# Graph layer with scattered sums: the last partial sums joined on VectorE, and the node stage in five lagged stages in source order

## The chip, the cores and the metric

The kernel runs on one core of a Trainium2 chip. A core has TensorE (PE) for matrix products, VectorE (DVE), ScalarE (ACT) and GpSimd (POOL) for element work, SyncE (SP), whose queue here only issues transfers, and 16 DMA engines that all queues share. Matrix products land in PSUM, everything else on the core lies in SBUF, and the tables of rows lie in device memory. The engines run side by side, each in the order of its own instructions, and wait for one another on semaphores. The metric is the device time of one execution in microseconds (us), as the median of several runs.

## The reference

One graph layer over 6,250 nodes with 64 features and 206,250 directed edges with 64 attributes: an MLP for each edge, the mean of its results at each edge's first node, an MLP for each node, a residual connection and a layer norm without weights.

```
msg  = concat([x[col], edge_attr])            # edges x 128
h    = relu(msg @ W1a.T + b1a) @ W1b.T + b1b  # 128 hidden, 64 out
agg  = segment_sum(h, row) / max(count, 1)
z    = relu(concat([x, agg]) @ W2a.T + b2a) @ W2b.T + b2b
out  = layernorm(x + concat([z, x]) @ Wr.T + br)
```

Everything is float32. `W1b` is linear and comes after the ReLU, so the kernel sums the 128 hidden values per node and folds `W1b`, `W2b` and `Wr` into combined weights (`wam_t`, `wzz_t`).

## The kernel before, in words

Nodes are split into 49 bins of 128 (the last has 106 nodes). Edges come in 124 blocks of 13 x 128. For each block PE forms the hidden values (line 949), ACT applies the ReLU (line 950), and POOL scatters the rows with 13 indirect DMAs (line 956) into a table in device memory that is sorted by bin. A row is 130 floats: 128 hidden values, a one that becomes the count, and the number of the node within its bin. A tile is 128 such rows.

The blocks are grouped into five epochs of 82, 17, 14, 7 and 4 blocks, each with a table of its own (three buffers in turn). When an epoch, or a step of the first one, is complete, its rows are read back (`read`, line 1000, on SP's queue, nine buffers `rt` in turn). DVE compares each row's node number with a ramp to form a one-hot matrix (`nodes_of`, lines 1031 and 1034), and PE multiplies one-hot by rows and so sums the rows of each node in PSUM (`summed`, line 1052). `sum_next` (line 1112) does this for a group of up to three bins: it sums the group, forms the next group's one-hot, and lets `collect` (line 1102) add all but the newest finished group into the SBUF array `part` with one DVE instruction (line 1110). The sums of the fourth epoch (seven blocks, three tiles per bin, two bins per group) are what is left after the last scatter, before the last step.

The last step (`last`, the fifth epoch) is treated in another way. Its bins have two tiles each, read three bins at a time. `sum_last` forms the one-hot and calls `summed` with `last` true. There the earlier sum of a bin is put into PSUM by an identity matmul ahead of the two tiles (line 1050), each bin in a PSUM tile of its own, so that PSUM ends with the complete sum. `finish` then takes over bin by bin: copy of the count (line 1286), reciprocal of the count (1288, 1289), scaling on ACT (1290), transpose on PE (1291). Every fourth bin `nodes` does the rest for four bins: copy of the transposed block on ACT (1299), the product with `wam_t` (1301), a maximum with the negated part that was computed long before (1302; that is the ReLU), four products with `wzz_t` (1305), the addition of the residual (1309), statistics (1313, 1314), square root on ACT (1316), reciprocal and offset (1317, 1319), normalisation on ACT (1323) and the output DMA on ACT's queue (1328, 1332).

Order: up to the end of the fourth epoch's sums, PE, ACT, DVE and SP run in source order (`in_order`, a manual schedule). The last step lies behind `in_order.close()`, where a planner orders each engine's instructions by its own estimates. Instructions behind the close that don't depend on the last step, such as the checks of line 805, are placed earlier by it. The checks end in `flag` (line 1373), which every engine loads before the kernel's last branch (lines 1427, 1428).

PSUM pools around the change: `spp` has two tiles for sums, `hp` three, which all node-stage products share in turn. The pool `nw` for the node stage's SBUF tiles has two of each.

Of the kernel before, what the change touches and what calls it, by code (L numbers as in the profile page):

```python
# [8 lines left out]
F32 = mybir.dt.float32  # L9
# [8 lines left out]
P = 128  # L18
# [459 lines left out]
def fast_path(  # L478
# [199 lines left out]
    with (  # L678
# [364 lines left out]
        def summed(st, reads, oh, of_bin, done):  # L1043

            last, at_tile = st is steps[-1], 0
            for b0, nb, t0, n, rt in reads:
                for j in range(nb):
                    b = b0 + j
                    if last and t0 == st.lo[b]:
                        nc.tensor.matmul(of_bin(b), ident, part[:, b, :], start=True, stop=False)  # L1050
                    for t in range(n):
                        nc.tensor.matmul(  # L1052
                            of_bin(b), oh[:, at_tile, :], rt[:, j * n + t, : H + 1],
                            start=t0 + t == st.lo[b] and not last, stop=t0 + t == st.hi[b] - 1,
                        )
                        at_tile += 1
                    if t0 + n == st.hi[b]:
                        done(b)
# [53 lines left out]
        def sum_next():  # L1112
# [5 lines left out]
            summed(g.st, g.reads, g.oh, lambda b: g.ps[:, b - g.b0, :], lambda b: None)  # L1118
            totals.append(g)
            mark()  # L1120
            collect(1)

# [147 lines left out]
        collect(0)  # L1270
        in_order.close()
# [4 lines left out]
        cnt_all = const.tile([P, NB], F32, name="cnt_all")  # L1276
        by_slot.close()
        with tc.tile_pool(name="nw", bufs=2) as nw:
            pending = []

            def finish(b, ps):
                if not pending:
                    pending.append((b, nw.tile([P, SUB, H], F32, name="agg"), hp.tile([P, SUB * P], F32, name="h_ps")))
                b0, agg, tr = pending[0]
                j = b - b0
                nc.vector.tensor_copy(cnt_all[:, b : b + 1], ps[:, H:])
                rc = nw.tile([P, 1], F32, name="rc")
                nc.vector.tensor_scalar(rc, ps[:, H:], 1.0, None, op0=ALU.max)
                nc.vector.reciprocal(rc, rc)
                nc.scalar.activation(agg[:, j, :], ps[:, :H], AF.Copy, scale=rc)  # L1290
                nc.tensor.transpose(tr[:, j * P : (j + 1) * P], agg[:, j, :], ident)
                if j == SUB - 1 or b == NB - 1:
                    nodes(b0, j + 1, tr)
                    pending.clear()

            def nodes(b0, n, tr):
                cols = slice(b0 * P, (b0 + n) * P)
                aT = nw.tile([P, SUB * P], F32, name="aT")
                nc.scalar.copy(aT[:, : n * P], tr[:, : n * P])
                p1 = hp.tile([P, SUB * P], F32, name="h_ps")  # L1300
                nc.tensor.matmul(p1[:, : n * P], wam_t, aT[:, : n * P], start=True, stop=True)  # L1301
                nc.vector.tensor_max(nq[:, cols], nq[:, cols], p1[:, : n * P])
                p3 = hp.tile([P, SUB, D], F32, name="h_ps")
                for j in range(n):
                    nc.tensor.matmul(  # L1305
                        p3[:, j, :], nq[:, (b0 + j) * P : (b0 + j + 1) * P], wzz_t, start=True, stop=True
                    )
                y = nw.tile([P, SUB, D], F32, name="y")
                nc.vector.tensor_add(y[:, :n, :], p3[:, :n, :], xr[:, b0 : b0 + n, :])
                st = nw.tile([P, SUB, 6], F32, name="st")  # L1310
                mvr = nw.tile([P, SUB, 2], F32, name="mvr")
                for j in range(n):
                    nc.vector.bn_stats(st[:, j, :], y[:, j, :])
                    nc.vector.bn_aggr(mvr[:, j, :], st[:, j, :])
                rstd = nw.tile([P, SUB], F32, name="rstd")
                nc.scalar.activation(rstd[:, :n], mvr[:, :n, 1], AF.Sqrt, bias=eps)
                nc.vector.reciprocal(rstd[:, :n], rstd[:, :n])
                off = nw.tile([P, SUB], F32, name="off")
                nc.vector.scalar_tensor_tensor(
                    off[:, :n], mvr[:, :n, 0], -1.0, rstd[:, :n], op0=ALU.mult, op1=ALU.mult  # L1320
                )
                for j in range(n):
                    nc.scalar.activation(  # L1323
                        y[:, j, :], y[:, j, :], AF.Identity, bias=off[:, j : j + 1], scale=rstd[:, j : j + 1]
                    )
                full = min(n, NF - b0)
                if full > 0:
                    nc.scalar.dma_start(
                        out[b0 * P : (b0 + full) * P].rearrange("(b p) f -> p b f", p=P), y[:, :full, :]
                    )  # L1330
                if full < n:
                    nc.scalar.dma_start(out[NF * P :], y[:REM, full, :])

            def sum_last():
# [96 lines left out]
```

## Time and profile before

| what | value |
|---|---|
| median of 9 runs | 2597.91 us (2587.15 to 2603.98) |
| the profiled execution | 2602.78 us |
| its span, first to last instruction | 2601.0 us |
| mean granted TensorE clock | 0.721 |
| busy PE / DVE / ACT / POOL | 1458.3 / 1181.4 / 327.0 / 1560.6 us |
| last scatter on POOL starts | 2452.47 us |
| first identity matmul (line 1050) | 2501.17 us |
| last output is issued (line 1332) | 2596.37 us |

Times inside the profile count from the start of the span. A line of a group view reads: source line, engine, operation, output<-inputs, shapes and count | busy us, mean ns of one | idle time of the engine just before them and what ended it. A line of the waits reads: who waited <- for whom: us in total, times, longest. A line of windows gives, for a stretch, the busy us of each engine with its instruction count, the granted TensorE clock (1.00 is full), the busy share of the DMA engines, and GB/s. In the page's slices each digit is a tenth. PE's float32 matmuls have two records each; PE's ends are modelled, so distances between starts say more than the lengths.

### The profile page before, as it was taken

To read this page: it belongs to the slowest core of one execution; us is meant where nothing else is said; L and a number is where in the kernel's file an instruction comes from. 1 tells how busy PE (TensorE), PEld (TensorE's weight loads), DVE (VectorE), ACT (ScalarE), POOL (GpSimd) and SP (SyncE) were. 2 spreads that over 40 slices of the span, in tenths; PEclk is the share of its full clock that TensorE was granted. 3 is DMA by queue.
4 is the path that set the end of the run, shared out by engine and by line. 5 is a ranking of instruction groups with operands and counts; after the bars stand their busy time and mean duration, and the time that the engine had idled before them with its cause. 6 is when DMAs were issued, how large, how long until landed. Compare 5 with 4: busy or idle time off the path is not lost.

```text
span 2601.0 us, 25280 instructions
## 1 busy us (share of the span) xinstructions
PE 1458.3 (56%) x8343; PEld 1277.3 (49%) x8343; DVE 1181.4 (45%) x2072; ACT 327.0 (13%) x799; POOL 1560.6 (60%) x1630
## 2 busy tenths in 40 slices
PE   3545553345545444544545566656656565667786
PEld 3434442344545334443444555555555554656775
DVE  5233343343443433344344444564554553555575
ACT  1111111101111101101110111111001010101024
POOL 6566666666666666666666666656666665665400
PEclk8666666666767766666667777776777776777799
DMA  7467655534444443433444555544555563555561
GB/s 169 132 224 255 171 161 162 154 115 114 135 117 130 119 113 114 125 115 112 135 119 123 149 152 147 161 134 139 149 147 152 150 173 111 159 164 170 183 186 29
DMA packets 198721, 375.23 MB, mean 144 GB/s; under 512 B 47034, under 2 KB 113916, under 8 KB 198452
## 3 DMA queue, kind: packets, MB, share of 16 engines
q1 hardware_dynamic: 114806, 222.07, 31.6%
q0 software_dynamic: 51584, 107.40, 13.1%
q10 hardware_dynamic: 32190, 44.05, 5.3%
q8 instruction: 68, 1.11, 0.2%
q14 instruction: 73, 0.60, 0.1%
HBM read 221.77 MB, written 151.59 MB: 144 GB/s over the span
## 4 chain that ended last, share of the span: by engine, by line
PE 26%; issue 16%; another core or an unknown queue 9%; DVE 5%; DMA 1%; ACT 1%; SPq 1%; ACTq 0%; DVEq 0%
PE sum_ps L1052 13%; PE h_ps L949 9%; DVE oh L1034 2%; DMA rt<-rows 1%; PE cnt_ps L851 1%; PE cnt_ps L850 1%; DVE rhs L929 1%; PE h_ps L1301 1%; DVE part L1110 1%; ACT y L1323 0%; PE h_ps L1305 0%; ACT orow L950 0%; DVE had L837 0%; DVE row L867 0%
## 5 line engine op out<-in xcount | busy, mean ns | idle before, releaser
L956 POOL DMA_INDIRECT rows<-orow,rowidx x1612 | 1552.7, 963 | 892.2 <-issue 457.0
L949 PE MATMUL h_ps<-mv,rhs 128*128 128x128 f32 x3224 | 632.5, 349 | 469.7 <-issue 339.0
L949 PEld LDWEIGHTS h_ps<-mv,rhs 128*128 128x128 f32 x3224 | 574.9, 259 | 535.2 <-issue 382.9
L1052 PE MATMUL sum_ps<-rt,oh 128*128 128x129 f32 x4006 | 621.9, 310 | 272.0 <-issue 247.3
L1052 PEld LDWEIGHTS sum_ps<-rt,oh 128*128 128x128 f32 x4006 | 578.4, 224 | 297.6 <-issue 272.3
L950 ACT ACTIVATE orow<-h_ps 128x512 f32<-128x512 f32 x496 | 248.9, 519 | 2069.8 <-remote 1191.6
L1034 DVE TENSOR_TENSOR oh<-ramp,rt 128x512 f32<-128x512 f32 (+3 forms) x213 | 144.9, 703 | 559.6 <-DMA rt<-rows 402.8
L929 DVE TENSOR_TENSOR rhs<-rhs,ramp 64x1664 f32<-64x1664 bf16 x116 | 219.4, 1892 | 20.3 <-DMA rhs<-relt 12.0
L837 DVE TENSOR_TENSOR_SCAN had<-ramp,bins 128x700 bf16<-128x700 bf16 x124 | 200.3, 1615 | 4.3
L1110 DVE TENSOR_TENSOR part<-part,sum_ps 128x258 f32<-128x258 f32 (+2 forms) x166 | 77.2, 465 | 269.3 <-remote 166.7
L850 PE MATMUL cnt_ps<-had,one_w 128*128 128x350 bf16 x248 | 100.2, 407 | 175.1 <-issue 87.9
L1034 DVE TENSOR_TENSOR oh<-ramp,node 128x512 f32<-128x512 f32 (+3 forms) x237 | 187.1, 790 | 7.3
L867 DVE TENSOR_REDUCE row<-cnt_ps 128x14 f32<-128x700 f32 x124 | 109.1, 880 | 105.9 <-issue 47.7
L1031 DVE SCALAR_TENSOR_TENSOR node<-unused,rt 128x4 f32<-128x4 bf16 (+3 forms) x237 | 37.4, 160 | 194.8 <-DMA rt<-rows 145.0
L851 PEld LDWEIGHTS <-before_w 128*128 128x128 bf16 x248 | 29.0, 117 | 196.8 <-issue 184.8
L851 PE MATMUL cnt_ps<-bins,before_w 128*128 128x325 bf16 x248 | 102.0, 414 | 37.0 <-issue 36.9
L831 DVE TENSOR_TENSOR bins<-ramp,hi 128x650 bf16<-128x650 f32 x124 | 108.2, 873 | 0.0
L850 PEld LDWEIGHTS <-one_w 128*128 128x128 bf16 x248 | 29.8, 120 | 74.7 <-issue 65.1
L1158 DVE TENSOR_SCALAR zT<-h_ps 128x512 f32<-128x512 f32 (+1 forms) x13 | 8.6, 661 | 121.1 <-remote 68.5
L1153 PE MATMUL h_ps<-zT,w2x_t 65*128 65x512 f32 (+1 forms) x26 | 20.4, 881 | 64.0 <-ACT orow L950 35.4
L830 DVE TENSOR_TENSOR bins<-had,ramp 128x50 bf16<-128x50 bf16 x119 | 44.1, 371 | 2.7
L1162 PE MATMUL h_ps<-nwzz_t,zT 128*128 128x64 f32 x98 | 22.5, 404 | 35.5 <-DVE zT L1158 20.7
(115 smaller groups left out, 445.2 us busy)
## 6 DMA issues: line engine op xcount, KB each, us to landing
rt<-rows SPq DMA_DIRECT2D x242, 260.0 KB
rhs<-in_edgeT SPq DMA_DIRECT2D x124, 416.0 KB
rt<-rows SPq DMA_DIRECT2D x106, 390.0 KB
rows<-orow,rowidx POOLq DMA_INDIRECT x1612
rhs<-relt SPq DMA_DIRECT2D x116, 208.0 KB
rows<-padrow ACTq DMA_DIRECT2D x4, 4680.0 KB
rows<-padrow ACTq DMA_DIRECT2D x8, 2340.0 KB
rt<-rows SPq DMA_DIRECT2D x48, 325.0 KB
```

Source lines behind the costliest of these rows:

```text
L831: nc.vector.tensor_tensor(by_bin[:, :, 1:], ramp[:, : 2 * HALF, None].to_broadcast([P, 2 * HALF, BLK]), hi[:, None, c0 : c0 + BLK].to_broa ...
L837: nc.vector.tensor_tensor_scan(had, on, oh, 0.0, op0=ALU.mult, op1=ALU.add)
L850: nc.tensor.matmul(v, one_w, had[:, b, :], start=True, stop=False)
L851: nc.tensor.matmul(v[:, :, :BLK], before_w, oh[:, b, 1:], start=False, stop=True)
L867: nc.vector.tensor_reduce(row, v.rearrange("p i b t -> p t i b"), axis=mybir.AxisListType.XY, op=ALU.max)
L929: nc.vector.tensor_tensor(rhs[D:, :].rearrange("p (h e) -> p h e", h=2), rel, in_win[D:, :, None].to_broadcast([WIN, 2, NG * P // 2]), op= ...
L949: nc.tensor.matmul(ps[:, j, :], rhs[:, c * P : (c + 1) * P], m, start=True, stop=True)
L950: nc.scalar.activation(orow[:, k0 : k0 + n, :H], ps[:, :n, :], AF.Relu)
L956: s = nc.gpsimd.indirect_dma_start(out=ep_.rows, out_offset=bass.IndirectOffsetOnAxis(ap=rowidx[:, t : t + 1], axis=0), in_=orow[:, j, :], ...
L1034: nc.vector.tensor_tensor(res[:, at_tile : at_tile + nb * n, :], ramp[:, None, :].to_broadcast([P, nb * n, P]), node[:, :, None].to_broadc ...
L1052: nc.tensor.matmul(of_bin(b), oh[:, at_tile, :], rt[:, j * n + t, : H + 1], start=t0 + t == st.lo[b] and not last, stop=t0 + t == st.hi[b] ...
L1110: nc.vector.tensor_add(to, to, g.ps[:, : g.nb, :])
```

## The change

The last step uses the same path as all others. `summed` loses the identity matmul, and `sum_next`, which now returns its group, sums the group's three bins in one PSUM tile; `collect` adds them to `part` with one DVE instruction for three bins. The reads of the last step go through `issue` and `to_issue` as all others do.

The node stage becomes a class `Nodes` with five methods for one group of up to three bins. Iteration i of the loop sums group i, collects group i-1, and then calls `means` for group i-1, `turned` for i-2, `layer` for i-3, `residual` for i-4 and `written` for i-5. `in_order.close()` moves behind this loop, so PE, ACT, DVE and SP take all of it in source order. The counts are read from `part` (three at a time for the reciprocals, all 49 at once for the final check). `nw` gets three buffers of each tile in place of two, and the outputs go to SP's queue.

```diff
-        def summed(st, reads, oh, of_bin, done):
+        def summed(st, reads, oh, of_bin):
...
-                    if last and t0 == st.lo[b]:
-                        nc.tensor.matmul(of_bin(b), ident, part[:, b, :], start=True, stop=False)
...
-                    if t0 + n == st.hi[b]:
-                        done(b)
...
             collect(1)
+            return g
...
-        collect(0)
-        in_order.close()
...
-        with tc.tile_pool(name="nw", bufs=2) as nw:
...
+        with tc.tile_pool(name="nw", bufs=3) as nw:
+            class Nodes:
...
+                def means(self):
+                    rc = nw.tile([P, SUMS], F32, name="rc")[:, : self.nb]
+                    nc.vector.tensor_scalar(rc, part[:, self.bins, H], 1.0, None, op0=ALU.max)
+                    nc.vector.reciprocal(rc, rc)
+                    self.agg = nw.tile([P, SUMS, H], F32, name="agg")
+                    for j in range(self.nb):
+                        nc.scalar.activation(
+                            self.agg[:, j, :], part[:, self.b0 + j, :H], AF.Copy, scale=rc[:, j : j + 1]
+                        )
+
+                def turned(self):
+                    tr = hp.tile([P, SUMS * P], F32, name="h_ps")
+                    for j in range(self.nb):
+                        nc.tensor.transpose(tr[:, j * P : (j + 1) * P], self.agg[:, j, :], ident)
+                    self.aT = nw.tile([P, SUMS * P], F32, name="aT")[:, : self.nb * P]
+                    nc.scalar.copy(self.aT, tr[:, : self.nb * P])
+
+                def layer(self):
+                    p1 = hp.tile([P, SUMS * P], F32, name="h_ps")[:, : self.nb * P]
+                    nc.tensor.matmul(p1, wam_t, self.aT, start=True, stop=True)
+                    nc.vector.tensor_max(nq[:, self.cols], nq[:, self.cols], p1)
+
+                def residual(self):
+                    p3 = hp.tile([P, SUMS, D], F32, name="h_ps")
+                    for j in range(self.nb):
+                        b = slice((self.b0 + j) * P, (self.b0 + j + 1) * P)
+                        nc.tensor.matmul(p3[:, j, :], nq[:, b], wzz_t, start=True, stop=True)
+                    y = self.y = nw.tile([P, SUMS, D], F32, name="y")
+                    nc.vector.tensor_add(y[:, : self.nb, :], p3[:, : self.nb, :], xr[:, self.bins, :])
...
+                    for j in range(self.nb):
+                        nc.vector.bn_stats(st[:, j, :], y[:, j, :])
+                    for j in range(self.nb):
+                        nc.vector.bn_aggr(self.mvr[:, j, :], st[:, j, :])
+
+                def written(self):
...
+                    nc.scalar.activation(rstd[:, :n], mvr[:, :n, 1], AF.Sqrt, bias=eps)
+                    nc.vector.reciprocal(rstd[:, :n], rstd[:, :n])
...
+                    for j in range(n):
+                        nc.scalar.activation(
+                            y[:, j, :], y[:, j, :], AF.Identity, bias=off[:, j : j + 1], scale=rstd[:, j : j + 1]
+                        )
...
+                        nc.sync.dma_start(
+                            out[b0 * P : (b0 + full) * P].rearrange("(b p) f -> p b f", p=P), y[:, :full, :]
+                        )
...
+            to_issue += [(last, g) for g in groups_of(last)]
+            n_last, on_way = len(to_issue), []
+            for i in range(n_last + 5):
+                issue(NGR)
+                if i < n_last:
+                    on_way.append(Nodes(sum_next()))
+                else:
+                    collect(0)
+                issue(NGR)
+                for lag, stage in enumerate(("means", "turned", "layer", "residual", "written"), 1):
+                    if 0 <= i - lag < n_last:
+                        getattr(on_way[i - lag], stage)()
+            in_order.close()
...
+            cnt_all = nw.tile([P, NB], F32, name="cnt_all")
+            nc.vector.tensor_copy(cnt_all, part[:, :, H])
```

## The prediction

> **What bounds the kernel now.** I read the page's slices first, to see which stage the change touches. A slice is 65.0 us.
>
> ```profile
> PE   3545553345545444544545566656656565667786
> ...
> POOL 6566666666666666666666666656666665665400
> PEclk8666666666767766666667777776777776777799
> ```
>
> Up to slice 38 the scatter on POOL runs without a break, and nothing in the diff reaches that part: the built order of POOL is the same in both kernels, and PE, DVE, ACT and SP differ there only in line numbers and in where a few small checks of 0.2 us sit. POOL's last scatter starts at 2452.47. All the change can do lies after it, and that stretch I read by windows (columns: bounds, length, busy us of PE, PE loads, DVE, ACT, POOL with counts, granted clock, DMA share, GB/s).
>
> ```profile
> 2456.00:2501.00 45.00, 43.75 (x365) 43.07 (x364) 41.69 (x110) 0.00 (x0) 0.00 (x0) 0.97 0.91 289
> 2501.00:2516.00 15.00, 10.43 (x74) 8.55 (x73) 8.44 (x51) 6.06 (x15) 0.00 (x0) 1.00 0.44 123
> 2516.00:2546.00 30.00, 23.22 (x159) 18.98 (x159) 18.93 (x111) 14.05 (x42) 0.00 (x0) 1.00 0.38 90
> 2546.00:2576.00 30.00, 23.93 (x152) 19.24 (x152) 17.87 (x103) 13.26 (x40) 0.00 (x0) 0.94 0.09 19
> ```
>
> From 2456 to 2501 the sums of the fourth epoch fill PE (97%) and DVE (93%): a full stage, which the change leaves alone. From 2501 PE is busy 77%, DVE 63%, ACT 47%, DMA below half: no engine is full. That is the last step, sums plus node stage. It runs from the first identity matmul (2501.17) to the issue of the last output (2596.37), 95.2 us for 49 bins. The starts of the square root, one per four bins, give its pace: 2521.76 to 2588.99 over nine periods, 7.47 us per four bins, 1.87 us per bin. What fills a period that no engine fills is the view of waits:
>
> ```profile
> DVE cnt_all L1286 <- PE sum_ps L1052: 13.1, 18, 1.4
> DVE zT L1302 <- PE h_ps L1301: 12.9, 11, 2.4
> ACT rstd L1316 <- DVE rc L1288: 11.2, 7, 1.8
> PE h_ps L1291 <- ACT agg L1290: 10.8, 12, 1.6
> ```
>
> PE waits for ACT, ACT for DVE, DVE for PE: one group of four goes through its whole chain with little of the next beside it. The last step is bound by hand-overs.
>
> **The change, part by part.** One period now handles three bins: 16 periods, and one for bin 48.
>
> *Removed.* The 98 records of the identity matmul (49 fp32 matmuls, two records each), and 49 each of the copy, the maximum and the reciprocal on DVE:
>
> ```profile
> L1034 DVE TENSOR_TENSOR oh<-ramp,node 128x768 f32<-128x768 f32 x15 | 14.2, 948 | 0.0
> ...
> L1289 DVE RECIPROCAL rc<-rc 128x1 f32<-128x1 f32 x49 | 7.7, 157 | 0.7
> L1286 DVE COPY cnt_all<-sum_ps 128x1 f32<-128x1 f32 x49 | 7.2, 147 | 13.1 <-PE sum_ps L1052 13.1
> ...
> L1110 DVE TENSOR_TENSOR part<-part,sum_ps 128x387 f32<-128x387 f32 x1 | 0.6, 560 | 0.3 <-PE sum_ps L1052 0.3
> ```
>
> *PE per period.* In the timeline four records of the sum take 0.45 us before the next begins, so 6 tiles, 12 records, 1.35. Three transposes at 0.11 make 0.35. The 512-column layer takes 0.96 until the next, so 384 columns 0.72. Six records of the residual at 0.118 make 0.70. Sum 3.1 us (before, the identity matmuls added 0.22 a bin).
>
> *DVE per period*, in issue order, each by the distance to the next start in the timeline: node places 0.20, one-hot 0.87, the added sum 0.56 plus 0.04 until its dependent starts, maximum and reciprocal 0.19 + 0.16. The layer's maximum has 128x384, between 0.69 (128x512) and 0.26 (128x128); nearest the first, 0.55, next start after 0.47. The residual's add 128x192, between 0.42 and 0.23, taken 0.36, dependent after 0.40. Three statistics and three aggregates 0.65 (four pairs took 0.87). Reciprocal and offset 0.40. Sum 3.94 us. So DVE, not PE, is the fullest engine; before, DVE had 63% of 5.6 us for three bins, 3.5 us: the added sum costs more than the copies that go.
>
> *ACT per period.* It adds nothing and loses the output DMAs. But source order makes a chain in one period: the reciprocal's start on DVE at 0.20 + 0.87 + 0.60 + 0.19 = 1.86; the mean starts 0.26 later (2579.21 to 2579.47), 2.12; three means 0.27 apart, 2.93; copy of the turned block, 384 columns, 0.49 of the 0.59 for 512, 3.42; square root, and its reciprocal on DVE 0.33 after its start (2593.12 to 2593.45), 3.75; the offset 0.21 later, 3.96; the next period's first DVE instruction about 0.1 after that. The last of these steps as the timeline has them before (start, length, engine):
>
> ```profile
> 2593.12 0.30 ACT L1316 ACTIVATE rstd<-mvr,eps 128x4 f32<-128x4 f32 x1 [1.07 <-DVE mvr L1314]
> ...
> 2593.45 0.18 DVE L1317 RECIPROCAL rstd<-rstd 128x4 f32<-128x4 f32 x1 [0.19 <-ACT rstd L1316]
> 2593.66 0.16 DVE L1319 SCALAR_TENSOR_TENSOR off<-mvr,rstd 128x4 f32<-128x4 f32 x1
> ```
>
> Behind that reciprocal DVE queues the next one-hot, and PE's next sums wait for it. The chain asks for 4.1, slightly over DVE's 3.94. The three normalisations (1.07 us) fall into the next period's first 1.3 us, before its means at 2.12, so they are covered; without that cover they would add 1.1 a period. PE's parts all use the previous period's results and fit before they are asked for. I take **4.1 us per period**; bounds are 3.6 (estimates of the two uncertain DVE shapes low, dependents as tight as independents) and 5.0 (each of nine hand-overs 0.1 longer).
>
> *Ramp.* Sums of group 0 can start where the identity matmul started, 2501.2. Its addition waits for 1.35 us of PE, 2502.7, and by DVE's growing share the first periods end at 2503.7, 2505.7, 2508.3, 2511.9. The next contains the activation table load (1.28 us at 2512.48 before; now ahead of the first square root too): 5.4, so 2517.3. Nine full periods: 36.9, 2554.2. The one before bin 48 has a small one-hot: 2557.8.
>
> *Drain.* Six periods without one-hots, worked the same way: 3.15, 2.95, 2.4, 2.2, 2.0, 2.6, sum 15.3, last output issued at 2573.1. Two waits are in that. The tiles for y are three deep, so the residual's add waits until the output of three groups before has landed; periods of 2 us bring that close: behind that add DVE queues the statistics and the previous group's offset, for which ACT waits. And in the built SP queue the load of the branch flag stands ahead of the last four outputs; the flag comes before their normalisation is over, and the load takes 0.28 + 0.15 + 0.02 us in the trace, so it costs nothing here, at most 0.5.
>
> How long an output needs is in the DMA view of 2582 to 2592 (40 slices of 0.25 us): an issue at 2583.99.
>
> ```profile
> GB/s 0 0 0 0 0 0 0 0 0 0 0 50 224 213 37 0 0 0 0 0 0 0 0 0 0 0 0 0 0 0 0 0 0 0 0 0 0 0 33 0
> ```
>
> Its bytes have moved by 2585.75, 1.75 us after issue; I use 1.9. [...]
>
> *Outputs moved to SP.* In the built order read 15 stands behind output 0 and read 16 behind output 1. Output 0 is ready in period 6, and read 15 is used in period 15: nine periods, 37 us, of cover; a read takes its data within a few us at 289 GB/s above. Last-step reads were all issued by 2538.8 before. Cost nothing; with the cover gone each would hold PE by one output's wait.
>
> *Clock.* One stretch speaks against the change:
>
> ```profile
> 2566.00:2567.50 1.50, 1.01 (x7) 0.82 (x7) 0.32 (x4) 1.50 (x5) 0.00 (x0) 1.00 0.00 0
> 2567.50:2569.00 1.50, 0.88 (x1) 0.42 (x2) 0.27 (x3) 1.18 (x4) 0.00 (x0) 0.75 0.31 62
> 2569.00:2570.50 1.50, 1.50 (x5) 0.93 (x4) 0.35 (x1) 0.00 (x0) 0.00 (x0) 0.50 0.13 25
> ```
>
> The grant halves for some 4 us, and four records of the sum take 0.86 instead of 0.45. [...] I take two such, 2 us in all.
>
> *Sum.* 2596.4 − 2573.1 = 23.3, less 2 for the clock: 21.3. From the last output's issue to the end it was 4.6 us, on queues and branches; taken unchanged, within 0.5. Span 2601.0 − 21.3 = 2579.7; the execution, 1.8 longer, 2581.4. The profiled run took 2602.78 and the median of the runs is 2597.91, so **2577 us** in the median.
>
> **Rivals.**
> - *Longer hand-overs*: period 5.0, ACT waiting for DVE and back. 12 full periods × 0.9 = 11 more: 2588. For it: four engines hand over in every period. Against: only the chain above closes within one period; all else has a period's slack.
> - *PE at half clock through the last step* (the other side): PE's 3.1 becomes 6.2 and sets the period. 12 × 2.1 = 25, and about 6 in ramp and drain, from 2575 without clock loss: 2606, slower. It decides from a mean period of 4.1 + 23.3/12 = 6.0 on. For it: the 0.50 row. Against: one such stretch in 95 us at the same share of PE.
> - *Ramp and drain take the gain*: they would have to take 23 us over the 16.1 and 15.3 counted, nearly twice as long, though each instruction in them is in the trace; or the end is set by PE's branch (3.9 us from 2593.9), which follows PE's last matmul and so moves along. 2598, no change.
>
> **How the numbers follow.** Main case 0.72, own range 2569 to 2585; longer hand-overs 0.15; half clock 0.07; no change 0.06. The range 2568 to 2592 takes in the 3.6 period (6 us less) and the hand-over case, and leaves out the last two and what lies under 2568. A measurement tells about 0.2% (5 us) from no change. Faster: main, hand-overs and a little of the others, 0.88; within 0.2% 0.05; slower 0.07.
>
> **What would show it.** Right: in the last step the square roots, one per three bins, stand 4.0 to 4.4 us apart; DVE is over 90% busy there; about 74 us from the last sums of the fourth epoch to the last output; no ACT wait for the mean over 1.5 us. Wrong: roots 5 us or more apart, with ACT's normalisation behind DVE or PE waiting for its copies; a grant near 0.5 for most of the step; DVE's y add held for DMA in the middle of the step and not only in the drain; or an end of the fourth epoch's sums other than about 2501.

## The result, and the profile after

The changed kernel takes 2572.15 us in the median of 10 runs (2569.18 to 2583.03), the kernel before on the same chip 2597.0 us in the median of 31 runs. The ratio of the two, from all their runs, is 0.9914, with a 95% interval of 0.99 to 0.9928 (the medians alone give 0.9904). The profiled execution took 2571.84 us, its span is 2570.1 us and its mean granted clock 0.714 (before: 2602.78, 2601.0 and 0.721).

The page's slices of the changed kernel, 64.3 us each: POOL ends two slices before the end as it did, and PE's last digit is 6 again. A slice is nearly as long as the whole last step, so this needs finer views.

```profile
PE   4745643445545445444555566665566565666796
POOL 6666666666666666666566665656666665666500
PEclk7656666667677767666676677777777786777798
```

The windows of the changed kernel (bounds, length, busy us of PE, PE loads, DVE, ACT and POOL with counts, granted clock, DMA share, GB/s) cut the end into the fourth epoch's sums, the ramp, a stretch of reduced clock, the steady part and the drain.

```profile
2448.00:2491.00 43.00, 41.78 (x354) 41.06 (x354) 39.91 (x100) 0.00 (x0) 0.96 (x1) 0.99 0.92 290
2491.00:2508.00 17.00, 16.74 (x133) 15.29 (x131) 14.13 (x45) 7.97 (x21) 0.00 (x0) 1.00 0.73 211
2508.00:2514.00 6.00, 4.23 (x19) 3.62 (x20) 5.48 (x21) 3.75 (x11) 0.00 (x0) 0.72 0.35 87
2514.00:2545.00 31.00, 27.13 (x188) 22.75 (x188) 27.65 (x119) 20.63 (x63) 0.00 (x0) 1.00 0.13 31
2545.00:2564.00 19.00, 9.55 (x51) 6.61 (x50) 12.28 (x72) 12.36 (x39) 0.00 (x0) 0.85 0.15 36
```

In the steady part DVE now has 89% and PE 88%; before, DVE had 63% and PE 77%. ACT has 67%. The fourth epoch's stage in front of it has the same character as before (PE 97%, DVE 93%, 290 GB/s), only earlier: the last step's first sums start at 2491.7 instead of 2501.2. The last scatter starts at 2448.25 instead of 2452.47, too, and POOL's order is the same in both kernels. I put this shift down to the two executions and not to the change: from the start of the last scatter to the first sums of the last step it is 43.4 us in the changed kernel and 48.7 before, but 48.9 in e1 below, which has the changed kernel's instructions up to there, and 43.5 in e2, which has the planner's order as before.

The waits of the changed kernel in the last step (who waited <- for whom: us in total, times, longest):

```profile
ACT agg L1288 <- DVE rc L1285: 14.2, 14, 2.1
ACT y L1328 <- DVE off L1324: 10.7, 17, 2.7
...
PE sum_ps L1050 <- DVE part L1106: 5.9, 8, 2.0
DVE rstd L1322 <- ACT rstd L1321: 5.7, 12, 1.6
DVE y L1310 <- DMA out_dram<-y: 3.0, 1, 3.0
```

The circle of before (PE for ACT, ACT for DVE, DVE for PE, over 10 us each) is gone. ACT and PE wait for DVE. DVE waits for ACT in one place, the square root, and once for an output DMA (for PE 0.9 us in all, at the step's two ends).

Where the 30.9 us between the two spans lie:

| part | before | after | difference |
|---|---|---|---|
| start to first sums of the last step | 2501.2 | 2491.7 | 9.5 |
| first sums to issue of the last output | 95.2 | 72.3 | 22.9 |
| issue of the last output to the end | 4.6 | 6.1 | -1.5 |

Only the last two rows belong to the change; they make 21.4 us. The medians are 24.9 us apart; the ratio makes 22.3 us of 2597.0, with 18.7 to 26.0 us inside the interval.

### The profile page after: what moved, and what is told of

It reads as the page before. It is cut to its first block, busy times and chain, and to the rows that moved or that the text cites. A ratio compares the mean times of both kernels' runs of the same rounds, so it can differ in the third digit from the quotient of the medians.

```text
span 2570.1 us, 25025 instructions
## 1 busy us (share of the span) xinstructions
PE 1459.2 (57%) x8253; PEld 1282.5 (50%) x8253; DVE 1184.3 (46%) x1993; ACT 326.9 (13%) x807; POOL 1555.3 (61%) x1630
## 4 chain that ended last, share of the span: by engine, by line
PE 24%; issue 15%; another core or an unknown queue 9%; DVE 5%; SPq 2%; DMA 1%; ACT 1%; ACTq 0%; DVEq 0%
PE sum_ps L1050 13%; PE h_ps L949 9%; DVE oh L1034 2%; DMA rt<-rows 1%; PE cnt_ps L850 1%; PE cnt_ps L851 1%; DVE part L1106 1%; DVE rhs L929 0%; ACT agg L1288 0%; SPq L918 0%; SPq L912 0%; SPq L1005 0%; DVE had L837 0%; DVE row L867 0%
## 5 line engine op out<-in xcount | busy, mean ns | idle before, releaser
L949 PEld LDWEIGHTS h_ps<-mv,rhs 128*128 128x128 f32 x3224 | 582.3, 262 | 529.4 <-issue 397.0
L1106 DVE TENSOR_TENSOR part<-part,sum_ps 128x258 f32<-128x258 f32 (+2 forms) x183 | 86.2, 472 | 272.4 <-remote 231.8
L1150 PE MATMUL h_ps<-zT,w2x_t 65*128 65x512 f32 (+1 forms) x26 | 21.4, 916 | 65.5 <-ACT orow L950 52.7
```

The lines of the kernel that those rows point to most:

```text
L949: nc.tensor.matmul(ps[:, j, :], rhs[:, c * P : (c + 1) * P], m, start=True, stop=True)
L1106: nc.vector.tensor_add(to, to, g.ps[:, : g.nb, :])
```

## The experiments

The experiments ran on three chips, on which the kernel before takes 2576.26 us (the first four experiments), 2172.82 us (the next four) and 2173.13 us (the last four), beside the 2597.0 us of the result above. On the last two, POOL waits less between its scatters: 501 us in the whole span, where it waited 893 us in the first profile of the changed kernel. The last step of the changed kernel is alike on both sides (69.6 and 70.6 us); the kernel before was traced on the first chip only. So runs are compared by their ratio to the kernel before on their own chip, and by the length of the last step in the trace, from the first mean on ACT to the issue of the last output: 93.05 us before (2503.32 to 2596.37), 69.6 us after (2494.43 to 2564.00). This length leaves out how early the first mean comes, which matters under e10. My theory at this point was that the written staging brings the gain, that the join by VectorE brings none, and that DVE's chain of dependents sets the period.

### e1: the five stages without a lag between them

```diff
-                for lag, stage in enumerate(("means", "turned", "layer", "residual", "written"), 1):
+                for lag, stage in ((1, s) for s in ("means", "turned", "layer", "residual", "written")):
```

> All five stages of a group run in the same iteration, one behind the sums; instructions, tiles and engines are those of the changed kernel. If hand-overs bound the last step and the lag is what hides them (main theory), one period is the whole chain: one-hot 1.07, added sum and reciprocal 0.95, means 0.9, transposes 0.5, copy 0.5, layer 0.8, maximum 0.55, residual 0.8, add and statistics 1.1, square root, reciprocal and offset 0.8, hand-overs 0.7: 8.7 us for three bins in place of 4.0, 17 periods, 76 us more, some 2648 us, slower than the kernel before by 50. If the gain comes from fewer, larger instructions and from the identity matmuls that are gone (rival), the lag is worth little: 2572 to 2585.

2644.36 us (two runs), ratio 1.0258 [1.0221, 1.0295]: slower than the kernel before. The last step takes 159.4 us, 9.8 us per three bins. A window of e1 over 120 us of that step, and PE in the timeline (start, length):

```profile
2490.00:2610.00 120.00, 82.69 (x280) 59.42 (x281) 45.97 (x184) 36.07 (x101) 0.00 (x0) 0.57 0.10 26
```

```profile
2487.05 2.89 PE L1050 MATMUL sum_ps<-rt,oh 128*128 128x129 f32 x12
...
2493.18 1.65 PE L1301 MATMUL h_ps<-aT,wam_t 128*128 128x384 f32 x2 [0.57 <-ACT aT L1297]
```

With one group going through all five stages in a row, every engine waits in turn, and the clock is at 0.57 of full over this window. The twelve records of the sum take 2.89 us, where they take 1.56 in the changed kernel. That is the half clock of the prediction's rival, with the waits in front of it; how much of the 9.8 us is the clock's, no run separates. In source order the lag is what carries the change.

### e2: the planner orders the new instructions

```diff
+        collect(0)
+        in_order.close()
         last = steps[-1]
...
-            in_order.close()
```

> The changed kernel with the manual schedule closed ahead of the last step, so that the planner orders the same instructions. If source order is what is needed, the planner brings back the hand-overs and the last step goes back toward 5.6 us for three bins: 2590 to 2600. If the lag written in the program is enough, the planner keeps the groups apart and the time is within 4 us of the changed kernel's 2572. Main theory takes the value between, 2580: in the built order the offset on DVE stands one add behind the reciprocal of the square root, which ACT waits for.

2547.17 us, ratio 0.9882 [0.9857, 0.9907]. The last step takes 56.4 us, 13 us less than in source order, with a mean of 2.92 us per three bins (square roots from 2489.60 to 2533.41, 15 periods). That was a miss: I had taken the planner for the slower one. By the time alone e2 is not told apart from the changed kernel (0.9914, on another chip: the intervals overlap); e10 settles it on one chip. A window of e2, and a part of DVE's timeline there:

```profile
2490.00:2520.00 30.00, 29.82 (x228) 26.36 (x227) 29.19 (x148) 25.04 (x79) 0.00 (x0) 1.00 0.23 61
```

```profile
2508.71 0.17 DVE L1324 RECIPROCAL rstd<-rstd 128x3 f32<-128x3 f32 x1
2508.80 0.14 DVE L1031 SCALAR_TENSOR_TENSOR node<-unused,rt 128x6 f32<-128x6 bf16 x1
2508.85 0.47 DVE L1316 BATCH_NORM_STATS2 st<-y 128x6 f32<-128x64 f32 x3
2509.24 0.30 DVE L1318 BATCH_NORM_AGGREGATE mvr<-st 128x2 f32<-128x6 f32 x3
2509.46 0.13 DVE L1326 SCALAR_TENSOR_TENSOR off<-mvr,rstd 128x3 f32<-128x3 f32 x1
2509.51 0.95 DVE L1034 TENSOR_TENSOR oh<-ramp,node 128x768 f32<-128x768 f32 x1
```

PE is busy 99% and DVE 97%. Between the reciprocal and the offset that needs it the planner has put other groups' work. In source order the two stand side by side.

### e3: the staging alone, with the identity join kept

```diff
+                    if last and t0 == st.lo[b]:
+                        nc.tensor.matmul(of_bin(b), ident, part[:, b, :], start=True, stop=False)
...
-                            start=t0 + t == st.lo[b], stop=t0 + t == st.hi[b] - 1,
+                            start=t0 + t == st.lo[b] and not last, stop=t0 + t == st.hi[b] - 1,
...
+                if g.st is steps[-1]:
+                    nc.vector.tensor_copy(part[:, g.b0 : g.b0 + g.nb, H], g.ps[:, : g.nb, H])
...
-                            self.agg[:, j, :], part[:, self.b0 + j, :H], AF.Copy, scale=rc[:, j : j + 1]
+                            self.agg[:, j, :], self.g.ps[:, j, :H], AF.Copy, scale=rc[:, j : j + 1]
```

> The staging alone: five lagged stages in source order, three bins in one PSUM tile, but the earlier sums go in by identity matmuls and the means are read from PSUM; DVE only copies the three counts. DVE loses 0.45 us of a period (3.94 to 3.5), PE gains 0.66 (3.1 to 3.8). Main theory (staging brings the gain, the join by VectorE costs DVE what it saves PE): period 3.8 to 4.1, 2566 to 2576. If the join carries a share of the gain: 2582 or more.

2552.73 us, ratio 0.9897 [0.9877, 0.9917]; last step 70.8 us, 3.87 us per period on average. In the window of e3 PE has become the fullest engine:

```profile
2505.00:2536.00 31.00, 29.70 (x232) 27.18 (x231) 25.72 (x120) 20.44 (x66) 0.00 (x0) 1.00 0.12 30
```

The identity matmuls take PE to 96%, and DVE, without the added sum of 0.55 us, falls to 83%. The period is a little shorter and the step as a whole a little longer than in the changed kernel. Once the stages are lagged, it makes no measurable difference which engine joins the parts. (Of the other parts of the change, three buffers in `nw` and the outputs on SP, none was tried alone; e3 has them too.)

### e4: the join alone, in the order and structure of before

```diff
-                oh, sums = nodes_of(last, reads), {}
-
-                def of_bin(b):
-                    if b not in sums:
-                        sums[b] = spp.tile([P, SUMS, H + 1], F32, name="sum_ps")[:, 0, :]
-                    return sums[b]
-
-                summed(last, reads, oh, of_bin, lambda b: finish(b, sums[b]))
+                oh = nodes_of(last, reads)
+                b0, nb = reads[0][0], reads[0][1]
+                ps = spp.tile([P, SUMS, H + 1], F32, name="sum_ps")
+                summed(last, reads, oh, lambda b: ps[:, b - b0, :], lambda b: None)
+                to = part[:, b0 : b0 + nb, :]
+                nc.vector.tensor_add(to, to, ps[:, :nb, :])
+                for b in range(b0, b0 + nb):
+                    finish(b, None)
```

The identity matmul is taken out of `summed`, and `finish` reads `part`.

> The join alone: the kernel before, with the earlier sums added by one DVE instruction for three bins and the bins finished from SBUF, four bins at a time, in the planner's order. Main theory: hand-overs stay, so the last step stays near 95 us: 2597 within 6. If the identity matmuls on PE and the wait of each bin for its PSUM tile were what bound it: 2585 or less.

2565.4 us, ratio 0.9957 [0.9939, 0.9976]: another miss. The last step takes 78.7 us (93 before) and 6.29 us per four bins (7.47 before). Two windows of e4, in front of and behind the end of its sums, and its waits:

```profile
2493.76:2525.42 31.66, 26.16 (x181) 21.11 (x181) 28.38 (x170) 19.76 (x58) 0.00 (x0) 1.00 0.15 36
2525.39:2551.09 25.70, 16.43 (x46) 9.84 (x46) 10.54 (x68) 12.67 (x36) 0.00 (x0) 0.50 0.13 27
```

```profile
ACT aT L1297 <- PE h_ps L1289: 12.5, 9, 3.7
DVE zT L1300 <- PE h_ps L1299: 9.3, 10, 2.9
DVE y L1307 <- PE h_ps L1303: 9.0, 10, 1.8
```

The waits that led the list of before, DVE's for the sums and PE's for the means, are not in its upper part any more. So in this step the staging alone is worth about 22 us and the join alone about 14, but both together 23.5. (By the medians, on the same chip, 23.5 and 10.9 us.) I read this as one circle of waits that either breaks up and that can be broken only once. The mean of 6.29 us hides two stretches. While sums are left, at full clock, six periods take 31.66 us, 5.28 us per four bins or 3.96 per three, with DVE 90% busy: the join alone has the pace of the changed kernel. From the first mean to the last record of the sums it is 51.9 us in e4 and 51.5 in the changed kernel, from there to the last output 26.8 and 18.1. So what the staging adds to the join shows at the end of the step, where e4 has more work left and runs at half clock; how much of the 8.7 us is the clock's is open. What in the join does it, e11 asks.

### e5 and e6: an instruction twice, on PE and on DVE

```diff
                     nc.tensor.matmul(p1, wam_t, self.aT, start=True, stop=True)
+                    nc.tensor.matmul(p1, wam_t, self.aT, start=True, stop=True)
```

> The changed kernel with the layer's product issued twice in every period (the second overwrites the first with the same values): 0.72 us more on PE. If DVE and the chain through ACT set the period (main theory), PE has 0.9 us of slack and the period stays at 4.0: within 3 us of the changed kernel. If PE or its hand-overs set it: 0.72 times 16 periods, 11 us more.

```diff
                     nc.vector.tensor_max(nq[:, self.cols], nq[:, self.cols], p1)
+                    nc.vector.tensor_max(nq[:, self.cols], nq[:, self.cols], p1)
```

> The changed kernel with the layer's maximum issued twice in every period (the second changes nothing): 0.44 us more on DVE, start to start. If DVE sets the period: 0.2 to 0.44 a period (0.23 of it may fall into DVE's wait for the square root), 3 to 7 us more. If hand-overs elsewhere set it: no change.

e5: 2147.81 us, ratio 0.9887 [0.9872, 0.9902], last step 71.5 us, square roots still 4.00 us apart. e6: 2149.58 us, ratio 0.9894 [0.9879, 0.991], last step 73.5 us, square roots 4.235 us apart. The same window of e5 shows how full PE then is:

```profile
2085.00:2113.00 28.00, 27.59 (x173) 22.12 (x174) 25.16 (x106) 18.54 (x56) 0.00 (x0) 1.00 0.18 45
```

PE took on 3.9 us in this window (23.70 in the same one of e9), 0.56 us a period, up to 98.5% busy, and nothing moved; the maximum on DVE added 0.24 us to the period. DVE's queue sets the pace, and PE had just under one layer product to spare. e6 adds less than the 0.56 us that the second maximum takes in DVE's timeline, because ACT's square root is then ready when DVE comes to its reciprocal: from the aggregate to the reciprocal it is 0.22 us there, and 0.53 in the changed kernel.

### e7: six tiles for y

```diff
-        with tc.tile_pool(name="nw", bufs=3) as nw:
+        with tc.tile_pool(name="nw", bufs=3) as nw, tc.tile_pool(name="yw", bufs=6) as yw:
...
-                    y = self.y = nw.tile([P, SUMS, D], F32, name="y")
+                    y = self.y = yw.tile([P, SUMS, D], F32, name="y")
```

> The changed kernel with six buffers for y in place of three. DVE waited 2.98 us in the drain for the output of three groups before. If nothing else is late there, the last step shortens by 2.5 to 3.0 us and no add of the residual waits for an output; if the flag's load or another hand-over is as late, by less than 1.

2142.77 us, ratio 0.9863 [0.9848, 0.9878]; last step 67.3 us, period unchanged (3.995). The wait of DVE for an output is gone, and the last three square roots stand 1.73 us apart (2130.30, 2132.03, 2133.76), where in the changed kernel the last stood 3.94 behind the one before. Beside e9, the changed kernel on a chip of the same speed (last step 70.6 us), the trace gives 3.3 us, a little more than expected.

### e8: the last stage first in the loop, with six tiles for y

```diff
-                for lag, stage in enumerate(("means", "turned", "layer", "residual", "written"), 1):
+                for lag, stage in ((5, "written"), (1, "means"), (2, "turned"), (3, "layer"), (4, "residual")):
```

> As the kernel with six buffers for y, and the stage that writes comes first in each iteration, so that ACT's square root is done before DVE asks for it. DVE waited 0.23 us for it in every steady period. Main theory: period 3.99 to 3.76, 12 periods, 2.8 us less, with the drain's 2.8 together 5 to 6 us under the changed kernel. If DVE's wait only moves to another instruction: 3 us under, as by the buffers alone.

2138.11 us, ratio 0.9839 [0.9826, 0.9853]; last step 60.8 us, period 3.52 us. I had expected 3.76, since only the wait for the square root (0.23 us) was to go. What came with it shows in DVE's timeline. First one period of the changed kernel, from one set of node places to the offset:

```profile
2520.08 0.16 DVE L1031 SCALAR_TENSOR_TENSOR node<-unused,rt 128x6 f32<-128x6 bf16 x1
2520.28 0.96 DVE L1034 TENSOR_TENSOR oh<-ramp,node 128x768 f32<-128x768 f32 x1
2521.16 0.55 DVE L1106 TENSOR_TENSOR part<-part,sum_ps 128x387 f32<-128x387 f32 x1
2521.74 0.17 DVE L1284 TENSOR_SCALAR rc<-part 128x3 f32<-128x3 f32 x1
...
2523.26 0.30 DVE L1316 BATCH_NORM_AGGREGATE mvr<-st 128x2 f32<-128x6 f32 x3
2523.79 0.18 DVE L1322 RECIPROCAL rstd<-rstd 128x3 f32<-128x3 f32 x1 [0.23 <-ACT rstd L1321]
2524.00 0.16 DVE L1324 SCALAR_TENSOR_TENSOR off<-mvr,rstd 128x3 f32<-128x3 f32 x1
```

The same place in e8:

```profile
2091.56 0.30 DVE L1316 BATCH_NORM_AGGREGATE mvr<-st 128x2 f32<-128x6 f32 x3
2091.78 0.14 DVE L1031 SCALAR_TENSOR_TENSOR node<-unused,rt 128x6 f32<-128x6 bf16 x1
2091.95 0.96 DVE L1034 TENSOR_TENSOR oh<-ramp,node 128x768 f32<-128x768 f32 x1
2092.82 0.55 DVE L1106 TENSOR_TENSOR part<-part,sum_ps 128x387 f32<-128x387 f32 x1
2093.29 0.17 DVE L1322 RECIPROCAL rstd<-rstd 128x3 f32<-128x3 f32 x1
2093.49 0.16 DVE L1324 SCALAR_TENSOR_TENSOR off<-mvr,rstd 128x3 f32<-128x3 f32 x1
2093.57 0.16 DVE L1284 TENSOR_SCALAR rc<-part 128x3 f32<-128x3 f32 x1
```

From the aggregate to the next instruction it is 0.22 us instead of 0.53. From the added sum to the next it is 0.47 instead of 0.58, since the next one no longer needs that sum. Behind the reciprocal the offset, which needs it, comes after 0.20 us; behind the offset an independent instruction comes after 0.08, in both kernels. In these places a DVE instruction behind the one whose result it needs starts about 0.1 us later than an independent one. The two shorter distances, 0.31 (of which 0.23 was the wait) and 0.11 us, make most of the 0.48 us of the period.

### e9: the changed kernel beside the last three

> The changed kernel as it is, beside the runs it is to be compared with. Ratio to before 0.991 (0.9895 to 0.993), first mean to last output 69.6 us (within 1), square roots 4.0 us apart: the chain of dependent instructions on DVE is the same on every chip.

2146.86 us, ratio 0.9881 [0.9866, 0.9897]; last step 70.6 us, square roots 4.00 us apart. The period repeats to 0.01 us; the ratio lies below the range that I had expected (0.9895 to 0.993). In microseconds the gain is 26.3; 22.3 with an interval of 18.7 to 26.0 was that of the first chip. Part of it is of another kind, as e10 shows.

### e10: the planner's order with six tiles for y

The edits of e2 and e7 together.

> The planner's order with the changed kernel's instructions, and a pool of six tiles for y. Theory: PE and DVE are full in the planner's order, so only the drain can gain: the wait for an output, 3 us in the changed kernel, goes; last step 53 to 56 us where the planner alone gave 56.4, ratio to before 0.986 to 0.988. Rival: the planner already keeps the outputs apart, so that no wait is left to take: ratio 0.988, last step 56 to 57.

2135.5 us, ratio 0.9827 [0.9813, 0.984]: 11.4 us below the changed kernel on the same chip and 37.6 below the kernel before. The ratio lies below both of the expected ranges. The last step takes 54.3 us, no wait for an output is left (e2 had one of 1.2 us), and the window is full again. This is the fastest version, ahead of both kernels.

```profile
2082.00:2112.00 30.00, 29.91 (x230) 26.69 (x229) 28.66 (x147) 25.54 (x79) 0.00 (x0) 1.00 0.25 62
2112.00:2128.50 16.50, 10.38 (x57) 7.88 (x55) 11.00 (x73) 12.29 (x40) 0.00 (x0) 0.79 0.20 45
```

How much of it the six tiles bring cannot be told: e2 ran on another chip, and the two last steps differ by 2.1 us only.

The last step is 16.3 us shorter than in e9, the whole run only 11.4. The rest is lost at the start. On the last two chips the fourth epoch's sums are nearly done long before the last scatter. In e9 they are done altogether (the last begins at 2037.8), and the last step's first sums begin 7.2 us after the last scatter starts (2056.99 to 2064.22). In e10 they begin 12.4 us after it (2057.56 to 2070.00), because in the planner's order DVE has node places of the last step ahead of the fourth epoch's last one-hot (128x384) and waits there for the last step's read:

```profile
2063.78 0.17 DVE L1031 SCALAR_TENSOR_TENSOR node<-unused,rt 128x6 f32<-128x6 bf16 x1 [28.54 <-DMA rt<-rows]
2064.95 0.17 DVE L1031 SCALAR_TENSOR_TENSOR node<-unused,rt 128x6 f32<-128x6 bf16 x1 [1.00 <-DMA rt<-rows]
2065.03 0.55 DVE L1034 TENSOR_TENSOR oh<-ramp,node 128x384 f32<-128x384 f32 x1
```

In e9 that one-hot ran at 2034.85. The other two runs with the planner's order on this chip (e11, e12) have the same wait and start 12.0 and 12.2 us after the scatter. The kernel before has the same order on DVE, so about 5 of the 26.3 us that source order gains on this chip probably lie there; no trace of it on this chip shows it. In the runs of the result and of e1 to e4 PE is still full with the fourth epoch's sums at that time, and the order cost nothing that the traces show.

The best order in source, e8, is not far behind: 2138.11 us on a chip of the same speed, 2.6 us above e10, and the intervals of the two ratios overlap (0.9839 [0.9826, 0.9853] and 0.9827 [0.9813, 0.984]).

### e11: the kernel before, with one PSUM tile for three bins

```diff
-                oh, sums = nodes_of(last, reads), {}
-
-                def of_bin(b):
-                    if b not in sums:
-                        sums[b] = spp.tile([P, SUMS, H + 1], F32, name="sum_ps")[:, 0, :]
-                    return sums[b]
-
-                summed(last, reads, oh, of_bin, lambda b: finish(b, sums[b]))
+                oh, b0 = nodes_of(last, reads), reads[0][0]
+                ps = spp.tile([P, SUMS, H + 1], F32, name="sum_ps")
+                summed(last, reads, oh, lambda b: ps[:, b - b0, :], lambda b: finish(b, ps[:, b - b0, :]))
```

> The kernel before with one edit: the three bins of a read share one PSUM tile, where each bin had one of its own; identity matmuls, single-bin copies and the planner's order stay. Theory A (the join by VectorE alone gained since it set the sums free of PSUM tiles held until the means were read): the pace goes from 7.5 us to about 6.3 per four bins, the last step from 93 to about 80 us, ratio about 0.995. Theory B (it gained since the 98 records of the identity matmul and the waits in front of them went): pace and ratio unchanged, 7.3 to 7.6 us and 0.999 to 1.001.

2198.38 us, ratio 1.0116 [1.0101, 1.0132], last step 122.6 us, 9.5 us per four bins. Neither theory had foreseen a loss. The waits of e11 in that step:

```profile
ACT agg L1290 <- DVE rc L1289: 39.1, 22, 3.6
PEld h_ps L1291 <- ACT agg L1290: 36.0, 25, 2.4
DVE cnt_all L1286 <- PE sum_ps L1052: 32.2, 24, 2.9
...
PEld sum_ps L1050 <- ACT agg L1290: 8.5, 8, 1.5
```

The last line was there before, with 2.0 us in 7 waits and at most 0.5: sums wait for ACT's mean of a bin in front of them, because that mean reads the tile they write. Here it has grown to 8.5 us. So the edit set the sums no freer; it tied each bin to the readers of the last one. The clock was lower too: it averages 0.84 over this step, and 0.98 over that of before; its share of the loss no run separates. What e11 shows is how much hangs on who reads the PSUM tile of the sums. With the readers of each bin one bin ahead in the same tile the pace is 9.5 us per four bins; with two tiles in turn (before) 7.47; with one DVE addition as the only reader (e4) 5.28 while sums are left. This speaks for theory A's mechanism but doesn't prove it: the identity matmuls that e4 also dropped had cost PE 0.22 us a bin, 0.9 us per four, and how much of e4's 2.2 us they carry stays open.

### e12: the planner, with the stages written without a lag

The edits of e1 and e2 together.

> The changed kernel's instructions with all five stages of a group written one after the other, and the planner orders them. Theory: the planner takes instructions by what is ready, so the written lag adds little: last step 56 to 60 us, ratio 0.988 to 0.990. Rival: what makes the planner's version fast is the lag in the order it is given; without it, it stands like the join alone: last step 75 to 80, ratio 0.995 to 0.997.

2141.82 us, ratio 0.9861 [0.9846, 0.9876]; last step 61.3 us (56 to 60 expected), square roots 3.4 us apart. In source order the same instructions without a lag took 159.4 us (e1). The planner finds the overlap that the source doesn't write down. The written lag and the deeper y pool together are worth 6.3 us more to it (e10, on the same chip); against e2, without the deeper pool but on another chip, the last step is 5 us longer.

## Why the prediction was right, and which of its terms were off

The forecast was 2577 us (2568 to 2592), the result is 2572.15. The last step was to take 71.9 us from its first sums to the last output, without the 2 us for the clock, and took 72.3. By its steps:

**Period, 4.1 us.** Measured 4.00 in two profiles of the changed kernel (the first runs from 2511.47 to 2535.45 in six periods). That DVE is fullest and PE has slack was right (e5, e6), but the slack is 0.6 us a period, the wait of PE for the added sum, and not 1.0. DVE's own work was put at 3.94 us and is 3.77; with the wait that follows it makes 4.00. That a chain through ACT lies slightly over DVE's work was right too: DVE waits 0.23 us in every period for the square root, and e8 takes this away. DVE at over 90% was not quite met: 89%, since of the 31 us of the steady window 1.9 went on the wait for the square root and 1.3 on gaps ahead of instructions that need the one in front of them. ACT's waits for the mean passed the 1.5 us that I had named as the limit twice, both in the ramp (1.75 and 2.08); in the steady part they are 0.91.

**Ramp.** From the first sums to the end of the period before bin 48's it was to take 56.6 us; with a period's end 0.7 us behind its square root (2547.17) it took 56.2.

**Drain, 15.3 us.** From that period's end to the last output it took 16.1, the sum of two errors of opposite sign. The y add of bin 48 waited for the output of three groups before:

```profile
2557.27 2.10 SPq L1333 DMA_DIRECT2D out_dram<-y  x2
...
2560.82 0.23 DVE L1310 TENSOR_TENSOR y<-h_ps,xr 128x64 f32<-128x64 f32 x1 [2.98 <-DMA out_dram<-y]
```

The term that was off is the landing time. I took 1.9 us, by the row of moved bytes, and the wait ends 3.55 us after the issue. By the DMA view of 2556.5 to 2561.5 (40 slices of 0.125 us) the bytes had moved by 2558.75, 1.5 us after the issue, so that 2.1 us more pass before the waiting engine goes on:

```profile
GB/s 66 0 0 0 0 0 0 0 0 0 0 0 0 66 215 211 187 256 0 0 0 0 0 0 4 8 8 115 223 221 205 49 2 0 0 0 0 0 0 0
```

So 0.9 us pass from the issue to the first byte, 0.6 us to the last, and 2.1 us from there to the waiting engine. The chain behind it was as told: DVE queued group 15's offset behind that add, and ACT waited 2.65 us for it. e7 removes the wait. The rest of the drain was quicker than worked out.

**Clock, 2 us for two stretches.** These 2 us were an estimate of mine, 1 us for each of two stretches like the one before, and no run shows them. While PE had work, one reduced stretch came, from about 2511 to 2514 (granted 0.50 to 0.53), and it followed a wait of PE for DVE in the period with the activation table load (a second came in the drain, from 2558 on, with PE's work done):

```profile
2509.77 2.27 PE L1050 MATMUL sum_ps<-rt,oh 128*128 128x129 f32 x12 [2.03 <-DVE part L1106]
```

The twelve records of that sum take 2.27 us and not 1.56. But the square roots went on 4.0 us apart (2507.48, 2511.47, 2515.47). PE's wait for the added sum, 0.61 us in the steady periods, was 0 and 0.15 us in the two that followed, so PE's slack covered it, and the cost was nothing. e9 is the comparison: the same wait of 2.02 us stands in the same place, the grant stays at full, and the square roots are just as far apart.

```profile
2084.89 1.61 PE L1050 MATMUL sum_ps<-rt,oh 128*128 128x129 f32 x12 [2.02 <-DVE part L1106]
```

In e6 and e7 the grant halved at that wait as in the changed kernel, between 0.2 us before its end and 1.3 us after it: the twelve records of the sum behind it take 2.95 us in e6 and 1.78 in e7, where the layer's product that follows takes 1.49 us and that of the next period 0.81. So the fall came with 2.0 us of idle on PE in three profiles of four. Why it failed to come in the fourth stays open.

**End, 4.6 us unchanged within 0.5.** It became 6.1, and 6.3 in e9: a miss of 1.5 us. Profiles with the outputs on ACT's queue have 4.6 (before), 4.9 (e4) and 4.8 us (e11), those with the outputs on SP 5.4 to 6.6. That the queue of the last output is the cause was not tried alone. **Outputs on SP past the reads** cost nothing, as expected: in the steady part no PE wait for a read is among the waits. **Upstream unchanged**: the profiled execution entered the last step 9.5 us earlier, at 2491.7, which I had named as a sign of being wrong; by e1 and e2 above it is a matter of the execution. The forecast of 2577 rests on the median, and 21.4 us of the last step with its end, against 21.3 forecast, leave 3.5 us of the 24.9 between the medians that no step accounts for, or 0.9 of the 22.3 by the ratio; the interval is wide enough for both. That 21.4 and 21.3 agree so well is luck: the ramp with its periods was 0.4 us and the clock 2 us better than forecast, the drain 0.8 and the end 1.5 us worse.

**Rivals.** Longer hand-overs (5.0 us) are excluded by the period. PE at half clock did happen, but in e1, where the grant was 0.57: there PE waits in every period (0.57 us for ACT's copy, 0.65 for DVE's maximum and about 1.7 for ACT's means), and how much of the 9.8 us its slower work makes no run separates. That ramp and drain eat the gain is excluded by their lengths.

What the prediction did not ask is whether source order was needed. I read the waits of before as a fault of the order, and they were in part one of the structure: e4 takes 14 us off the last step with the order of before, and leaving the order of the new instructions to the planner takes 13 us more off than source order does (e2), of which some 5 us can be lost again at the start (e10). My theory that the join brings nothing and that the written order is what helps fell with these two.

## What to carry to other kernels

When two edits break up the same circle of waits, each alone may bring most of what both bring together; test them one at a time before crediting either. In an order written by hand look for the two things that cost time here: an engine that sets the pace and takes dependents back to back (4.00 us a period in the changed kernel, 3.52 in e8), and buffers that wait for an output and are too few for the fastest periods, those of the drain (3.3 us of the last step, e7 beside e9). Before freezing an order by hand, run the same instructions through the planner: here the new structure was worth more with it than with the order first written for it, and a second order written by hand (e8) came within 2.6 us of it. And measure such a stage from an event that the order cannot move: from the first mean the planner's version looks 16.3 us better than source order, from the last scatter 11.2.

## What the runs showed of the hardware that was not expected

- A dependent DVE instruction started about 0.1 us later than an independent one: 0.58 (changed kernel) against 0.47 us (e8) behind the same 128x387 addition, 0.20 against 0.08 behind instructions on 128x3 (e8).
- An output of 96 KB on SP's queue released its buffer 3.55 us after the issue, 2.1 us after the last byte had moved (changed kernel).
- The granted clock halved around the end of a PE wait of 2.0 us in the changed kernel, in e6 and in e7, and did not at the same wait in e9. It averaged 0.57 over 120 us in which PE waited 0.6 to 2.0 us at a time (e1). In the changed kernel the halving cost nothing: the square roots stayed 4.0 us apart, as in e9. What the low clock makes of e1's 9.8 us a period no run separates.
- The kernel before takes 2597, 2576, 2173 and 2173 us in the four sets of runs. POOL's busy time is nearly the same in the profiles (1560.6 us in the first profile of before, 1555.9 in e9); what differs most is how long it stands between scatters: 893 us in the first profile of the changed kernel and 501 in e9, 392 of the 425 us between the two spans.
